# Query projections in two full column blocks instead of four padded ones, moved to their partitions by DMA

## The chip, the core and the metric

The kernel runs on one NeuronCore of a Trainium2 chip. Five engines work from instruction queues of their own: TensorE (PE, with its weight loads shown as PEld), VectorE (DVE), ScalarE (ACT), GpSimd (POOL) and SyncE (SP), which issues most of the DMAs. The metric is the device time of one execution, in microseconds (us). "Span" is the time from the first to the last instruction in the profiler's record of one execution.

## What is computed

The reference is one transformer layer in float32, with layer norms after each half: attention with 16 query heads and 4 key-value heads, then a mixture of 8 experts (one for each token) beside a shared one. Two sequences of 1024 tokens, 256 channels.

```python
q = (x @ Wq).reshape(B, T, N_HEAD, HEAD_DIM).transpose(0, 2, 1, 3)      # B 2, T 1024, 16 heads of 16
k = (x @ Wk).reshape(B, T, N_HEAD_KV, HEAD_DIM).transpose(0, 2, 1, 3)   # 4 heads of 16, repeated 4 times
v = (x @ Wv).reshape(B, T, N_HEAD_KV, HEAD_DIM).transpose(0, 2, 1, 3)
att = jnp.einsum('bhqd,bhkd->bhqk', q, k) * scale + alibi[None] + causal[None, None]
y = jnp.einsum('bhqk,bhkd->bhqd', jax.nn.softmax(att, axis=-1), v)
x = _layernorm(x + y.transpose(0, 2, 1, 3).reshape(B, T, C) @ Wo)
# each token goes to the expert with the largest logit; xr is x times its sigmoid
x = _layernorm(x + silu(x @ sh_gate) * (x @ sh_up) @ sh_down
                 + (up(xr) * silu(gate(xr))) @ down_proj)
```

## The kernel before

**Layout of queries and keys.** A head has 16 numbers, but a score matmul works on a quadrant of 32 partitions. Quadrant g (partitions 32 g to 32 g + 31) belongs to key-value head g. Row 0 of a quadrant carries the position term: the query side holds the head's slope (qbias), the key side the position (kaug). Row 1 is for the row maximum, rows 16 to 31 hold the head's 16 numbers. qT is 128 partitions x 4 (r, the query head within its group) x 1024 tokens; kT is 128 x 1024. To get this layout straight out of a matmul, the weights are padded: wq_pad (L129) has, for each r, 4 groups of 32 columns of which 16 are filled, so that one r gives 128 columns; wk_pad is the same for the keys.

**Projections by halves.** A half is 512 tokens of one batch; there are four. For each half, turn_x (L305) transposes x into xT with 8 matmuls and one copy on ScalarE; do_kv (L316) projects keys and values, and VectorE adds kaug (L330) and ScalarE copies the values (L331); do_q (L333) projects the queries for two values of r, and ScalarE writes them with the bias into qT (L338). So a half takes two calls of do_q, and each writes two blocks of 128 columns, in two matmuls each. All of these tiles, and those of the scores, come from one PSUM pool, ps_st, with 3 buffers of two banks.

**Order.** On PE, VectorE, ScalarE and GpSimd the order in the attention part is that of the program text (MANUAL); on SP it is a scheduler's there, and the program's in the expert part. Ahead of the attention part stands a setup, which a scheduler orders: the loads, the padded weights, rowsel, slopes, qbias and kaug (L147 to L158).

**Stages of the attention part.**

- first_projections (L354): two matmuls of zeros, the transposes of the first half, do_kv and both calls of do_q for it, and turn_x of the second half.
- Ten lead steps (LEAD): each computes the scores of one unit (start_s, two bursts of matmuls, L401) and reduces them to row maxima (end_s: VectorE on L416, L425 and L444, ScalarE on L432 with GpSimd on L433). They cover the query tiles 0 to 3 of batch 0. Between them stand pieces of the projections of the other three halves, taken from the list of projections() (L342) by weight: after step k, pieces are taken until their share left is at most (9 - k) / 10.
- The main steps: for each query tile and key tile, transposed scores with the maximum subtracted (t_ps, L481), exponentials on ScalarE (L500), the product with the values (L524), and one unit of scores further on; join_maxima and spread_maxima (L451, L461) bring the maxima from the one to the other, with qS = qT + mT on VectorE (L469).
- The shared expert (sh_gu, sh_d) and the routing fill the end of it; routed rows are scattered into slot_x in DRAM. Then comes the expert part.

**Loads.** On SP in this order: x (xs, four parts), wo, the router, the shared expert's weights (L110 to L112, 1.5 MB) and a fill of slot_x with an empty row (L281, 3.9 MB). ScalarE issues those of Wq, Wk and Wv.

**Buffers.** The pool "probT" has four buffers under the tag pT, 8 KB a partition, for probabilities; xT of batch 1 takes one of them until its projections are done.

Of the kernel before, what the change touches and what calls it, by code (L numbers as in the profile page):

```python
# [9 lines left out]
F32 = mybir.dt.float32  # L10
# [6 lines left out]
P = 128  # L17
# [13 lines left out]
    mybir.EngineType.DVE,  # L31
    mybir.EngineType.Activation,
    mybir.EngineType.Pool,
}


# [8 lines left out]
def attn_moe_postln_kernel(  # L45
# [61 lines left out]

    sh_gu = const.tile([P, KC, F2], F32, tag="sh_gu", name="sh_gu")
    sh_d = const.tile([P, FC, C], F32, tag="sh_d", name="sh_d")
    nc.sync.dma_start(out=sh_gu[:, :, :FF], in_=sh_gate.rearrange("(c p) f -> p c f", p=P))  # L110
    nc.sync.dma_start(out=sh_gu[:, :, FF:], in_=sh_up.rearrange("(c p) f -> p c f", p=P))
    nc.sync.dma_start(out=sh_d, in_=sh_down.rearrange("(c p) n -> p c n", p=P))  # L112

# [9 lines left out]

    wq_pad = acon.tile([P, KC, REP, N_KV, PAD], F32, tag="wq_pad", name="wq_pad")
    wk_pad = acon.tile([P, KC, N_KV, PAD], F32, tag="wk_pad", name="wk_pad")  # L129
    nc.vector.memset(wk_pad, 0.0)  # L130
    nc.vector.memset(wq_pad, 0.0)
    for c in range(KC):
        nc.vector.tensor_scalar_mul(
            wq_pad[:, c, :, :, ROW_HEAD : ROW_HEAD + HD],
            wq_raw[:, c, :].rearrange("p (g r d) -> p r g d", g=N_KV, d=HD),
            scale,
        )
        nc.vector.tensor_copy(
            wk_pad[:, c, :, ROW_HEAD : ROW_HEAD + HD],
            wk_raw[:, c, :].rearrange("p (g d) -> p g d", d=HD),  # L140
        )
# [121 lines left out]
    with (  # L263
# [11 lines left out]
    ):  # L275
        qT, kT, xT = {}, {}, {}

        empty = shp.tile([P, ROW], F32, tag="th", name="empty")
        nc.gpsimd.memset(empty, 0.0)
        nc.gpsimd.memset(empty[:, NUM : NUM + 1].bitcast(I32), NTT * P)  # L280
        nc.sync.dma_start(out=slot_xt, in_=empty.unsqueeze(1).broadcast_to([P, SLOTS // P, ROW]))  # L281


        def pj_tile(name):
            return ps_m.tile([P, 512], F32, tag="m", name=name)
# [1 line left out]
        def own_tiles(b, xTb):  # L287
            xT[b] = xTb
            kT[b] = qkp.tile([P, T], F32, tag="kT", name=f"kT_{b}")
            qT[b] = qkp.tile([P, REP, T], F32, tag="qT", name=f"qT_{b}")  # L290

        def project(dst, b, w, cols):
            for c in range(KC):
                nc.tensor.matmul(  # L294
                    dst, lhsT=w(c), rhs=xT[b][:, c, cols], start=(c == 0), stop=(c == KC - 1)
                )

        def wq_of(r):
            return lambda c: wq_pad[:, c, r].rearrange("p g d -> p (g d)")

        def wk_of(c):
            return wk_pad[:, c].rearrange("p g d -> p (g d)")
# [2 lines left out]
        def turn_x(b, i):  # L305
            if b not in xT:

                xTb = ptp.tile([P, KC, T], F32, tag="pT", name=f"xT_{b}")
                own_tiles(b, xTb)
            tp = ps_st.tile([P, KC, 512], F32, tag="st", name="xtp")  # L310
            for c in range(KC):
                for j in range(4):
                    nc.tensor.transpose(tp[:, c, ts(j, P)], xs[:, b * QT + i + j, ts(c, P)], ident)
            nc.scalar.copy(xT[b][:, :, i * P : (i + 4) * P], tp)
# [15 lines left out]
            nc.vector.tensor_add(kT[b][:, cols], pj[:, 0], kaug[:, cols])  # L330
            nc.scalar.copy(vs[b][:, i : i + 4, :, 0:HD], pv)  # L331

        def do_q(b, r, i):  # L333
            cols = slice(i * P, (i + 4) * P)
            pj = ps_st.tile([P, 2, 512], F32, tag="st", name="qpj")
            for j in range(2):
                project(pj[:, j], b, wq_of(r + j), cols)
            nc.scalar.activation(qT[b][:, r : r + 2, cols], pj, AF.Identity, bias=qbias)  # L338

        halves = [(b, i) for b in range(B) for i in range(0, QT, 4)][1:]  # L340

        def projections():  # L342


            pieces = []
            for h, after in zip(halves, [*halves[1:], None]):
                pieces.append((11, lambda h=h: do_kv(*h)))
                pieces.append((14, lambda h=h: do_q(h[0], 0, h[1])))
                if after:
                    pieces.append((4, lambda h=after: turn_x(*h)))  # L350
                pieces.append((14, lambda h=h: do_q(h[0], 2, h[1])))
            return pieces

        def first_projections():  # L354

            own_tiles(0, xTp.tile([P, KC, T], F32, tag="xT", name="xT_0"))
            cols = slice(0, 512)
            warm = ps_st.tile([P, 2, 512], F32, tag="st", name="warm")
            zeros = mnegs[0].rearrange("p r g d -> p (r g d)")
            for i in range(2):  # L360
                nc.tensor.matmul(warm[:, i], lhsT=zeros[:, :P], rhs=zeros, start=True, stop=True)
            tp = ps_st.tile([P, KC, 512], F32, tag="st", name="xtp0")
            for c in range(KC):
                for j in range(4):
                    nc.tensor.transpose(tp[:, c, ts(j, P)], xs[:, j, ts(c, P)], ident)
            nc.scalar.copy(xT[0][:, 0, cols], tp[:, 0])
            nc.vector.tensor_copy(xT[0][:, 1, cols], tp[:, 1])
            do_kv(0, 0)
            do_q(0, 0, 0)
            do_q(0, 2, 0)  # L370
            turn_x(*halves[0])


        def s_units(b, qt):
# [464 lines left out]
        for k in range(LEAD):  # L839
            unit = s_queue.pop(0)  # L840
            sps = [start_s(unit, h) for h in range(2)]
            run(*[m for _, m in sps])
            for h in range(2):
                end_s(unit, h, sps[h][0], h == 1)
            while fill and left * LEAD > total * (LEAD - 1 - k):
                left -= fill[0][0]
                fill.pop(0)[1]()
            gap(0)
        for n, (b, qt, kt) in enumerate(steps):
            last = n + 1 == len(steps) or steps[n + 1][:2] != (b, qt)  # L850
            made = []
            if kt != qt:
                made.append((2 * n + 2, (b, qt, kt, kt == 0, False)))
            if last:
                ready = max(2 * n + 2, 2 * first[b, qt] + (7 if qt >= 3 else 4))
                made.append((ready, (b, qt, qt, qt == 0, True)))
            if s_queue:
                unit = s_queue.pop(0)
                for h in range(2):
                    t = start_t(b, qt, kt, h)  # L860
                    s = start_s(unit, 1 - h)
                    run(t[1], s[1])
                    end_t(b, qt, kt, h, t[0])
                    end_s(unit, 1 - h, s[0], h == 1)
                    if h == 1:
                        products += made
                    gap(6)
            else:

                t = [start_t(b, qt, kt, h) for h in range(2)]  # L870
                run(t[0][1], t[1][1])
                for h in range(2):
                    end_t(b, qt, kt, h, t[h][0])
                products += made
                wide_gap()
# [13 lines left out]
    with (  # L889
# [6 lines left out]
        tc.tile_pool(name="ps_d", bufs=2, space=PSUM) as ps_d,  # L896
        tc.tile_pool(name="ps_t", bufs=2, space=PSUM) as ps_t,
        tc.tile_pool(name="rt2", bufs=1) as rtp,
        tc.manual_schedule(engines=MANUAL | {mybir.EngineType.SP}),
    ):  # L900
        wgu = wgup.tile([P, E, KC, F2], F32, tag="wgu", name="wgu")
        wd = wgup.tile([P, E, FC, C], F32, tag="wd", name="wd")
# [386 lines left out]
```

## Time and profile before

| | us |
|---|---|
| median of 3 runs | 615.26 (612.56 to 615.57) |
| the profiled execution, its time | 613.16 |
| the profiled execution, its span | 611.4 |
| span from 0 to 19.8: setup and first projections, PE busy | 16.3 of 19.8 |
| 19.8 to 71.5: lead steps, PE / DVE / ACT busy | 49.6 / 31.0 / 16.1 of 51.7 |
| 71.5 to 350: main steps, PE / DVE / ACT busy | 272.9 / 194.3 / 167.1 of 278.5 |
| 350 to 460: last steps and shared expert, PE busy | 102.7 of 110.0 |
| 460 to the end: expert part, PE busy | 133.1 of 151.4 |

A busy share says how long an engine had an instruction at work, and matmuls are pipelined, so that a busy PE may still be waiting within an instruction. What decides a stage is which wait ends last there; that is read from the chain, which follows each piece of work back to what released it. In the views of the chain and the timeline, a line has its start, its length (both us), the engine, the tile and the line of the kernel, and the number of instructions. In the groups, a line has the count, the total busy us and the mean ns of one, then the idle time ahead of it and what ended most of that.

### The profile page before, as it was taken

The numbers are of one execution on the slowest core, as the hardware profiler recorded it, in microseconds if no ns is written. First come the engines' busy times: TensorE is split into PE (matmuls) and PEld (weight loads), VectorE is DVE, ScalarE is ACT, GpSimd is POOL, SyncE is SP. The second block draws the span as 40 slices with busy tenths as digits, with TensorE's granted clock in tenths as the row PEclk, the third lists the DMA queues.
The fourth block names the chain that finished last, engine by engine and source line by source line (L and its number), as shares of the span: only waits on it lengthen the run. The fifth ranks groups of instructions, "written<-read, shape, count | busy, mean of one in ns | idle before, by whom it ended". The sixth has DMA issues, their size and how long they took to land.

```text
span 611.4 us, 9157 instructions
## 1 busy us (share of the span) xinstructions
PE 574.6 (94%) x3708; PEld 321.0 (53%) x3708; DVE 334.0 (55%) x606; ACT 253.5 (41%) x313; POOL 155.2 (25%) x189
## 2 busy tenths in 40 slices
PE   7999999999999999999999999998989999999990
PEld 4555434444445353435355634545554788888660
DVE  3275667857675766676766834343442254454541
ACT  1423476565665655646465664453112111111120
POOL 3010222111111102013312120222102147767541
PEclk9999989999999999999999999999999999999996
DMA  9700000000000000001100000100053345752100
GB/s 310 236 1 2 1 0 2 2 1 1 1 1 2 1 1 0 3 0 36 36 1 2 2 0 1 52 19 18 17 206 102 118 177 177 260 198 69 57 22 4
DMA packets 23102, 32.65 MB, mean 53 GB/s; under 512 B 3294, under 2 KB 18948, under 8 KB 23056
## 3 DMA queue, kind: packets, MB, share of 16 engines
q1 hardware_dynamic: 18784, 25.28, 12.5%
q0 software_dynamic: 3456, 6.34, 3.0%
q8 instruction: 31, 0.51, 0.4%
q10 hardware_dynamic: 816, 0.39, 0.2%
q14 instruction: 15, 0.12, 0.1%
HBM read 22.20 MB, written 12.97 MB: 58 GB/s over the span
## 4 chain that ended last, share of the span: by engine, by line
PE 84%; DVE 6%; ACT 5%; issue 1%; DMA 1%; POOL 0%; POOLq 0%; ACTq 0%
PE t_ps L481 15%; PE s_ps L401 12%; PE yT L524 11%; PE gu_sh L683 6%; PE qpj L294 5%; PE gp L1100 5%; PE dp L1116 5%; PE up L1100 5%; PE dp_sh L703 3%; ACT pT L500 3%; PE o_ps L569 2%; DVE past L416 2%; PE mT L465 1%; PE dp L1158 1%; PE gp L1008 1%
## 5 line engine op out<-in xcount | busy, mean ns | idle before, releaser
L416 DVE TENSOR_REDUCE past<-s_ps 128x2 f32<-128x1024 f32 (+2 forms) x112 | 136.5, 1223 | 71.2 <-PE s_ps L401 71.0
L401 PE MATMUL s_ps<-kT,qT 32*128 32x128 f32 (+2 forms) x1280 | 154.0, 379 | 4.2 <-ACT pT L500 2.0
L500 ACT ACTIVATE pT<-t_ps 128x1024 f32<-128x1024 f32 x112 | 113.9, 1025 | 94.5 <-PE s_ps L401 59.8
L481 PE MATMUL t_ps<-qS,kT 32*128 32x512 f32 x576 | 149.0, 633 | 0.9 <-DVE qS L469 0.8
L401 PEld LDWEIGHTS s_ps<-kT,qT 32*128 32x128 f32 x1280 | 79.9, 185 | 36.2 <-ACT pT L500 25.2
L481 PEld LDWEIGHTS t_ps<-qS,kT 32*128 32x128 f32 x576 | 41.3, 183 | 52.0 <-issue 30.1
L504 POOL TENSOR_SCALAR_AFFINE_SELECT pD<-pD 128x1024 f32<-128x1024 f32 x32 | 34.7, 1091 | 103.2 <-ACT pD L502 103.1
L524 PE MATMUL yT<-pT,v 128*32 128x512 f32 x448 | 59.7, 605 | 0.0
L433 POOL TENSOR_SCALAR_AFFINE_SELECT diag<-diag 128x1024 f32<-128x1024 f32 x16 | 17.5, 1091 | 135.4 <-ACT diag L432 123.0
L233 POOL TENSOR_TENSOR rstd<-rstd,neg_half 128x1 f32<-128x1 f32 x36 | 20.5, 570 | 121.5 <-DVE rstd L232 119.4
L683 PE MATMUL gu_sh<-x1T,sh_gu 128*128 128x512 f32 x96 | 43.8, 598 | 1.9 <-DVE h_sh L695 1.3
L239 POOL DMA_INDIRECT slot_x<-xs,slots x32 | 32.1, 1002 | 43.7 <-DVE slots L664 27.7
L502 ACT COPY pD<-t_ps 128x1024 f32<-128x1024 f32 x32 | 32.1, 1017 | 25.6 <-PE s_ps L401 19.9
L444 DVE TENSOR_REDUCE past<-diag 128x8 f32<-128x1024 f32 x32 | 38.6, 1210 | 0.0
L516 ACT ACTIVATE pD<-pD 128x1024 f32<-128x1024 f32 x32 | 33.6, 1056 | 0.3 <-POOL pD L504 0.3
L1108 ACT ACTIVATE sg<-gp 128x512 f32<-128x512 f32 x16 | 9.6, 597 | 54.6 <-PE gp L1100 47.1
L692 DVE SCALAR_TENSOR_TENSOR h_sh<-th,gu_sh 128x512 f32<-128x512 f32 x12 | 8.3, 688 | 43.0 <-ACT th L691 43.0
L1100 PE MATMUL gp<-slot_xT,wgu 128*128 128x256 f32 x128 | 30.4, 381 | 1.2 <-ACT slot_xT L1069 1.2
L1100 PE MATMUL up<-slot_xT,wgu 128*128 128x256 f32 x128 | 30.2, 379 | 0.0
L294 PE MATMUL qpj<-xT,wq_pad 128*128 128x512 f32 x64 | 29.2, 602 | 0.6
L1116 PE MATMUL dp<-wd,slot_h 128*128 128x256 f32 x128 | 29.0, 379 | 0.0
L683 PEld LDWEIGHTS gu_sh<-x1T,sh_gu 128*128 128x128 f32 x96 | 17.4, 190 | 20.4 <-issue 17.2
(170 smaller groups left out, 675.2 us busy)
## 6 DMA issues: line engine op xcount, KB each, us to landing
wgu<-_L_ffn_gate_up_proj_dram SPq DMA_DIRECT2D x8, 1024.0 KB
wd<-in_L_ffn_down_proj_dram SPq DMA_DIRECT2D x8, 512.0 KB
slot_x<-empty SPq DMA_DIRECT2D x1, 3900.0 KB
row<-slot_x SPq DMA_DIRECT2D x8, 260.0 KB
xs<-in_L_attn_x_dram SPq DMA_DIRECT2D x4, 512.0 KB
z_dram<-z_sh SPq DMA_DIRECT2D x12, 128.0 KB
row<-slot_x SPq DMA_DIRECT2D x4, 130.0 KB
sh_gu<-L_ffn_shared_gate_w_dram SPq DMA_DIRECT2D x1, 512.0 KB
```

The source lines that it names most:

```text
L294: nc.tensor.matmul(dst, lhsT=w(c), rhs=xT[b][:, c, cols], start=(c == 0), stop=(c == KC - 1))
L401: lambda r=r, j=j, rows=rows: nc.tensor.matmul(sp[:, j, r * n * P : (r + 1) * n * P], lhsT=qT[b][rows, r0 + r, ts(qt, P)], rhs=kT[b][rows, ...
L416: nc.vector.tensor_reduce(past[:, gs, r0 : r0 + nr, parts[b, qt][key]], sp.rearrange("p j (r k) -> p j r k", r=nr), AX.X, ALU.max, negate= ...
L444: lambda: nc.vector.tensor_reduce(past[:, gs, :, 0], diag[:, gs], AX.X, ALU.max, negate=True),
L481: lambda j=j, rows=rows: nc.tensor.matmul(tp[:, j, :], lhsT=kT[b][rows, ts(kt, P)], rhs=qS[b, qt][rows].rearrange("p r q -> p (r q)"), sta ...
L500: nc.scalar.activation(p, tp, AF.Exp)
L504: nc.gpsimd.affine_select(out=p, in_=p, pattern=[[0, HALF * REP], [1, P]], compare_op=ALU.is_ge, fill=MASKED, base=0, channel_multiplier=-1,)
L516: lambda: nc.scalar.activation(p, p, AF.Exp),
L524: nc.tensor.matmul(yTs[b, qt][g * PAD : (g + 1) * PAD], lhsT=vs[b][:, kt, g, :], rhs=p[:, g, :], start=start, stop=stop,)
L683: nc.tensor.matmul(gu[:, k], lhsT=sh_gu[:, c, col : col + P], rhs=x1T[:, c, ts(tb, TB)], start=(c == 0), stop=(c == KC - 1),)
L1100: nc.tensor.matmul(dst[:, j], lhsT=wgu[:, e, c, col : col + P], rhs=xT[:, c, :], start=(c == 0), stop=(c == KC - 1),)
L1116: nc.tensor.matmul(dp, lhsT=h[:, f, ts(i, P)], rhs=wd[:, e, f, :], start=(f == 0), stop=(f == FC - 1),)
```

## The change

The query weights lose their padding: wq_r holds, for each value of r, 4 groups of 16 columns, so that two values of r make one block of 128 columns. do_q projects a half's queries in one call of two such blocks. Their rows come out as (r, g, 16 numbers), not in the quadrants of qT. They are copied to an SBUF tile (stage, a pT buffer; in the first half ScalarE and VectorE copy one block each), and eight DMAs on SP, one for each of two r and four g, bring 16 partitions each to rows 16 to 31 of quadrant g in qT. The bias row and the zero rows of qT are written beforehand, by a copy of qbias over the whole tile, 512 tokens at a time: by ScalarE for the first half, by GpSimd for the others (own_tiles).

In first_projections the query projection comes ahead of do_kv, and do_kv of the second half is added at its end. The list of pieces has one call of do_q a half, and do_kv of the second half is out of it. The loads of the shared expert's weights and the fill of slot_x, with the two GpSimd memsets that it needs, are issued after the lead steps. SP follows the program's order in the attention part too.

```diff
@@ -31,6 +31,7 @@
     mybir.EngineType.DVE,
     mybir.EngineType.Activation,
     mybir.EngineType.Pool,
+    mybir.EngineType.SP,
 }
 
 
@@ -107,9 +108,6 @@
 
     sh_gu = const.tile([P, KC, F2], F32, tag="sh_gu", name="sh_gu")
     sh_d = const.tile([P, FC, C], F32, tag="sh_d", name="sh_d")
-    nc.sync.dma_start(out=sh_gu[:, :, :FF], in_=sh_gate.rearrange("(c p) f -> p c f", p=P))
-    nc.sync.dma_start(out=sh_gu[:, :, FF:], in_=sh_up.rearrange("(c p) f -> p c f", p=P))
-    nc.sync.dma_start(out=sh_d, in_=sh_down.rearrange("(c p) n -> p c n", p=P))
 
 
 
@@ -125,13 +123,13 @@
 
 
 
-    wq_pad = acon.tile([P, KC, REP, N_KV, PAD], F32, tag="wq_pad", name="wq_pad")
+
+    wq_r = acon.tile([P, KC, REP, N_KV, HD], F32, tag="wq_r", name="wq_r")
     wk_pad = acon.tile([P, KC, N_KV, PAD], F32, tag="wk_pad", name="wk_pad")
     nc.vector.memset(wk_pad, 0.0)
-    nc.vector.memset(wq_pad, 0.0)
     for c in range(KC):
         nc.vector.tensor_scalar_mul(
-            wq_pad[:, c, :, :, ROW_HEAD : ROW_HEAD + HD],
+            wq_r[:, c],
             wq_raw[:, c, :].rearrange("p (g r d) -> p r g d", g=N_KV, d=HD),
             scale,
         )
@@ -275,11 +273,6 @@
     ):
         qT, kT, xT = {}, {}, {}
 
-        empty = shp.tile([P, ROW], F32, tag="th", name="empty")
-        nc.gpsimd.memset(empty, 0.0)
-        nc.gpsimd.memset(empty[:, NUM : NUM + 1].bitcast(I32), NTT * P)
-        nc.sync.dma_start(out=slot_xt, in_=empty.unsqueeze(1).broadcast_to([P, SLOTS // P, ROW]))
-
 
         def pj_tile(name):
             return ps_m.tile([P, 512], F32, tag="m", name=name)
@@ -288,6 +281,10 @@
             xT[b] = xTb
             kT[b] = qkp.tile([P, T], F32, tag="kT", name=f"kT_{b}")
             qT[b] = qkp.tile([P, REP, T], F32, tag="qT", name=f"qT_{b}")
+            for i in range(0, T, 512):
+
+                copy = nc.scalar.copy if b == 0 and i == 0 else nc.gpsimd.tensor_copy
+                copy(qT[b][:, :, i : i + 512], qbias.unsqueeze(2).broadcast_to([P, REP, 512]))
 
         def project(dst, b, w, cols):
             for c in range(KC):
@@ -295,8 +292,8 @@
                     dst, lhsT=w(c), rhs=xT[b][:, c, cols], start=(c == 0), stop=(c == KC - 1)
                 )
 
-        def wq_of(r):
-            return lambda c: wq_pad[:, c, r].rearrange("p g d -> p (g d)")
+        def wq_of(m):
+            return lambda c: wq_r[:, c, 2 * m : 2 * m + 2].rearrange("p r g d -> p (r g d)")
 
         def wk_of(c):
             return wk_pad[:, c].rearrange("p g d -> p (g d)")
@@ -330,12 +327,27 @@
             nc.vector.tensor_add(kT[b][:, cols], pj[:, 0], kaug[:, cols])
             nc.scalar.copy(vs[b][:, i : i + 4, :, 0:HD], pv)
 
-        def do_q(b, r, i):
+        def do_q(b, i):
+
+
             cols = slice(i * P, (i + 4) * P)
+            stage = ptp.tile([P, N_KV, 512], F32, tag="pT", name="q_all")[:, :2]
             pj = ps_st.tile([P, 2, 512], F32, tag="st", name="qpj")
-            for j in range(2):
-                project(pj[:, j], b, wq_of(r + j), cols)
-            nc.scalar.activation(qT[b][:, r : r + 2, cols], pj, AF.Identity, bias=qbias)
+            for m in range(2):
+                project(pj[:, m], b, wq_of(m), cols)
+            if (b, i) == (0, 0):
+                nc.scalar.copy(stage[:, 0], pj[:, 0])
+                nc.vector.tensor_copy(stage[:, 1], pj[:, 1])
+            else:
+                nc.scalar.copy(stage, pj)
+            to = qT[b].rearrange("p (m r) t -> p r m t", r=2)
+            for r in range(2):
+                for g in range(N_KV):
+                    row = (r * N_KV + g) * HD
+                    nc.sync.dma_start(
+                        out=to[g * PAD + ROW_HEAD : g * PAD + ROW_HEAD + HD, r, :, cols],
+                        in_=stage[row : row + HD],
+                    )
 
         halves = [(b, i) for b in range(B) for i in range(0, QT, 4)][1:]
 
@@ -344,11 +356,11 @@
 
             pieces = []
             for h, after in zip(halves, [*halves[1:], None]):
-                pieces.append((11, lambda h=h: do_kv(*h)))
-                pieces.append((14, lambda h=h: do_q(h[0], 0, h[1])))
+                pieces.append((14, lambda h=h: do_q(*h)))
                 if after:
                     pieces.append((4, lambda h=after: turn_x(*h)))
-                pieces.append((14, lambda h=h: do_q(h[0], 2, h[1])))
+                if h != halves[0]:
+                    pieces.append((11, lambda h=h: do_kv(*h)))
             return pieces
 
         def first_projections():
@@ -365,10 +377,10 @@
                     nc.tensor.transpose(tp[:, c, ts(j, P)], xs[:, j, ts(c, P)], ident)
             nc.scalar.copy(xT[0][:, 0, cols], tp[:, 0])
             nc.vector.tensor_copy(xT[0][:, 1, cols], tp[:, 1])
+            do_q(0, 0)
             do_kv(0, 0)
-            do_q(0, 0, 0)
-            do_q(0, 2, 0)
             turn_x(*halves[0])
+            do_kv(*halves[0])
 
 
         def s_units(b, qt):
@@ -846,6 +858,16 @@
                 left -= fill[0][0]
                 fill.pop(0)[1]()
             gap(0)
+
+        nc.sync.dma_start(out=sh_gu[:, :, :FF], in_=sh_gate.rearrange("(c p) f -> p c f", p=P))
+        nc.sync.dma_start(out=sh_gu[:, :, FF:], in_=sh_up.rearrange("(c p) f -> p c f", p=P))
+        nc.sync.dma_start(out=sh_d, in_=sh_down.rearrange("(c p) n -> p c n", p=P))
+
+        empty = shp.tile([P, ROW], F32, tag="th", name="empty")
+        nc.gpsimd.memset(empty, 0.0)
+        nc.gpsimd.memset(empty[:, NUM : NUM + 1].bitcast(I32), NTT * P)
+        nc.sync.dma_start(out=slot_xt, in_=empty.unsqueeze(1).broadcast_to([P, SLOTS // P, ROW]))
+
         for n, (b, qt, kt) in enumerate(steps):
             last = n + 1 == len(steps) or steps[n + 1][:2] != (b, qt)
             made = []
@@ -896,7 +918,7 @@
         tc.tile_pool(name="ps_d", bufs=2, space=PSUM) as ps_d,
         tc.tile_pool(name="ps_t", bufs=2, space=PSUM) as ps_t,
         tc.tile_pool(name="rt2", bufs=1) as rtp,
-        tc.manual_schedule(engines=MANUAL | {mybir.EngineType.SP}),
+        tc.manual_schedule(engines=MANUAL),
     ):
         wgu = wgup.tile([P, E, KC, F2], F32, tag="wgu", name="wgu")
         wd = wgup.tile([P, E, FC, C], F32, tag="wd", name="wd")
```

## The prediction

> **What bounds the kernel now.** First the page, for who is busy: PE in every slice, and the chain that ends last is 84% PE, with the query projections among its parts.
>
> ```profile
> PE 574.6 (94%) x3708; PEld 321.0 (53%) x3708; DVE 334.0 (55%) x606; ACT 253.5 (41%) x313; POOL 155.2 (25%) x189
> PE 84%; DVE 6%; ACT 5%; issue 1%; DMA 1%; POOL 0%; POOLq 0%; ACTq 0%
> L294 PE MATMUL qpj<-xT,wq_pad 128*128 128x512 f32 x64 | 29.2, 602 | 0.6
> ```
>
> Reader: 64 records for 8 calls of do_q, so 8 a call; their ends overlap, and a call holds PE 3.43 us (below: 6.92 for two).
>
> Second, the chain over the start, 0 to 21 us.
>
> ```profile
> 1.29 5.74 DMA wk_raw<-in_L_attn_Wk_dram
> ...
> 7.06 0.30 DVE wk_pad L138 x2
> ...
> 7.73 0.72 DVE kaug L158
> 8.45 0.06 DVE qbias L153
> 8.52 0.61 DVE xT L367
> 9.13 0.04 issue
> 9.17 1.12 PE kvpj L294 x2
> 10.29 1.73 PE kvpj L323 x16
> 12.03 6.92 PE qpj L294 x16
> 18.95 0.88 PE xtp L313 x8
> ```
>
> VectorE takes everything behind the landing of wk_raw; qbias is ready only at 8.5. The first score burst (S0) starts at 19.8.
>
> Third, the chain from 17 to 76 us, the ten lead steps.
>
> ```profile
> 31.94 1.18 DVE past L416
> 33.12 0.04 issue
> 33.16 3.71 PE qpj L294 x8
> 36.88 0.02 issue
> 36.90 1.12 ACT qT L338
> 38.02 0.04 issue
> 38.07 1.99 PE kvpj L294 x4
> ```
>
> Every query block is on it. PE to ACT to PE means one of the three PSUM pairs ("st") is returned. They go round in program order: a score burst takes two, a projection or turn one.
>
> **The skill.** "DMA: Bandwidth & Descriptors", Anatomy of one DMA: about 2 us fixed for a transfer, mostly the receipt. No row of before is a transfer inside SBUF; SP's issue of a load is 0.35 to 0.6 us there. "SBUF — State Buffer", Door 1: 16 partitions reach 4 of 16 ports, 104 GB/s measured. "TensorE: Matmul & The Clock Gate", Part 1: an idle window of 3.4 us can halve the clock. The trace agrees on the cold side: the first L361 records take 0.86 us where L294 ones take 0.43. "SBUF — State Buffer", Who interferes with whom: tensor_reduce never contends with GpSimd; the trace can't show it yet.
>
> **Projections.** Four heads of 16 columns padded to 32 filled a 128-column block; now eight fill it, so a half needs two blocks instead of four. Eight do_q of 3.43 become four: -13.7 us of PE. In the first half that is -3.43, in the lead -10.3. One more kv projection (3.47: 1.72 + 1.75) goes from the lead to before S0.
>
> **The start.** In after, ACT's first work is the fill of qT: 128x2048 from qbias. From the COPY rows (512 in 0.585, 1024 in 1.01) a 2048 copy is 1.87. It waits for qbias, 8.5, and behind it in ACT's order stands the copy of xT's first half, at 6.48 in before. So: fill 8.55 to 10.45, xT to 11.05, PE idle since 6.44. I take VectorE's order as before: the removed memset of wq_pad (0.91) lay in the wait for wq_raw. Then do_q 11.05 to 14.5, do_kv to 18.0, turn_x to 19.05. The added do_kv needs that turn's xT: ACT 1.1, so it runs 20.2 to 23.7; rps, and S0 at 23.9: +4.1 against 19.8.
>
> **Transfers.** The stage copies (0.58 ACT, 0.68 DVE, side by side) end at 15.25. SP issues eight transfers of 64 KB at 0.45, to 18.9; with 2.2 for the last one's landing (2 fixed, 0.6 by 104 GB/s lying partly in it) 21.1. That is 2.8 inside S0's 23.9, hence free. Cover gone: each transfer would have to hold the queue 0.8 instead of 0.45. Bounds: below 0 is excluded, since S0 waits for PE anyway; above, 1.5 each gives S0 at 29.5 (+5.6). SP also waits eight DMAs back: rw_raw is issued at 4.97, 1.2 after the issue before it, on wq_raw by SP's list of waits. By 15.3 the loads are down, as the later ones (sh, slot_x) now come after the lead. The other 24 transfers serve queries not read in the lead, and nothing on SP is due then.
>
> **The lead.** ACT's evacuations go from six of 1.11 to three of 1.01. I lay the instructions out with before's durations (S 1.15, reduces L416 1.22 and L444 1.21, diag 1.22, do_kv 3.47, turn 1.05), the three PSUM pairs and the new list. Costs now sum to 72, so steps 0 to 8 take q(0,4); turn(1,0); q(1,0); none; turn(1,4); kv(1,0); q(1,4); none; kv(1,4). Times from S0's start: S0 0 to 1.2; q to 4.65; S1 to 5.8; turn to 6.9; S2 to 8.3; q to 11.75; S3 to 12.95. S4 waits for S3's diag on VectorE, 14.5. Turn to 16.7; S5 waits for S4's reduce, 18.15; kv 19.3 to 22.75; S6 to 23.9; q to 27.4; S7 to 28.55; S8 waits, 29.85; kv 31.1 to 34.55; spread_maxima; S9 35.2 to 36.4. VectorE: 12 reduces of scores (14.7), 8 of diag (9.7), 4 diag (4.9), two kT, one qS and two joins (2.4): 31.7 (the trace has 31.0 in 19.8 to 71.5); its waits (1.25 at S0, 3.4 for S1 behind q, 1.1 for kv, 2.7 for S7) 8.4: join at 40.1. In before the second join ends at 71.5, 51.7 after S0. So the lead gives 51.7 - 40.1 = 11.6: of 13.8 taken from PE (10.3 and 3.5), 2.2 goes to waits for VectorE, late next.
>
> **GpSimd and the rest.** Three fills of 2048, by its affine_select (1024 in 1.09) about 2.1 each; up to 4.4 each if twice as slow. The two of batch 1 start at about 8 after S0 and end by 12.3 (17 at worst); the next diag select comes at 14.1, and its result is reduced only at 23.5: free. Tiles of pT for stages: four buffers, first probabilities after the lead: free. Late loads: sh_gu is read from 355, slot_x scattered into at about 275; 5.4 MB took some 20 us in before: free. From the main steps on the order is the same, and PE is busy 48.8 of 50 us, so what the lead ends earlier is the end earlier.
>
> **Sum.** +4.1 - 11.6 = -7.5. The profiled execution has a span of 611.4 and a time of 613.16: it would have 605.7. The median, 615.26, is 2.1 above it; the same step from it gives 607.8. I forecast 608.
>
> **Rivals.** (1) qbias comes early: ident is ready at 3.24, so if VectorE takes rowsel, slopes and qbias before the weights, the fill ends at about 6.2 and xT's copy is not late. q then ends at 10.7, S0 starts at 20.1, gain 11.3: 604. Against it: VectorE sat idle until 5.06 with ident ready at 3.24 and still took wk_pad first. (2) PE's pause (4.6 us) or the thinner lead costs the clock. For: the page's PEclk falls to 8 around 80 us. Half speed for one or two windows is 1.7 to 3.4, and as much in the lead where VectorE doesn't cover it: gain 3 to 5, 611. (3) VectorE binds the lead harder, or the first steps at 70 to 90 us fall into a worse phase: gain under 3, 614. To lose 4.5 more, PE would have to stall half a step in each of ten. (4) Slower: the transfers. If each holds the queue for its whole life instead of being issued over the last, S0 comes at 15.25 + 8p + 2. It passes 23.9 at p = 0.8; the gain is gone when S0 is 7.5 later, p = 1.8; slower by over 3 us from p = 2.1. At p = 2.3 S0 is at 35.7, and the time 615.3 - 7.5 + 11.8 = 620. For: a fixed 2 us each, few ports, eight waits of PE on eight transfers. Against: SP issued loads 0.5 apart without waiting for landings. (5) The change doesn't do as it says: a score burst could wait for transfers into other columns of qT. In before S3 starts at 36.79 while ACT writes other columns of qT from 36.90, so reads are kept apart by region; I give it nothing of its own.
>
> **Numbers.** Forecast 0.50, (1) 0.14, (2) 0.13, (3) 0.09, (4) 0.14. A measurement of this kernel tells 0.5% from nothing, about 3 us. Faster: 0.50 + 0.14 + 0.13 = 0.77; same 0.09; slower 0.14. The range leaves out (4) and the edges of (1): 602.5 to 615. The likeliest case's own range is 605 to 611 (profiled time or median as the base; 2 us of clock or landing).
>
> **What would show it.** Right: qpj with 32 records; S0 at 23 to 25 us with PE, not a DMA, before it; the fill of qT on ACT from 8.5 to 10.4; S0 to the second join some 40 us; VectorE named ahead of S4, S5, S8; from there to the end as before. Wrong: s_ps waiting on DMA qT, 128x512 records of 0.86 after 11 us, a fill at 4 us (rival 1), or a main part longer than before.

## The result, and the profile after

The changed kernel takes 608.07 us (median of 4 runs, 607.72 to 609.49) where the kernel before, measured beside it, takes 615.41 (4 runs, 612.56 to 616.83). The ratio is 0.9891, 95% interval 0.9852 to 0.993: some 7 us faster, as forecast. The profiled execution of after took 608.26 us with a span of 606.6.

The page of after, its busy times, the granted clock of TensorE over 40 slices of some 15 us, the chain by engine and the issues of the new transfers:

```profile
PE 566.0 (93%) x3676; PEld 318.6 (53%) x3676; DVE 333.5 (55%) x606; ACT 250.3 (41%) x310; POOL 161.2 (27%) x192
...
PEclk8999799999999999999999999999999999999997
...
PE 82%; DVE 6%; ACT 5%; issue 2%; DMA 1%; SPq 1%; POOL 0%; POOLq 0%; ACTq 0%; DVEq 0%
...
qT<-q_all SPq DMA_DIRECT2D x32, 64.0 KB, 2.3
```

PE has 32 matmuls fewer: 8 instead of 16 for each of four halves. That is the removed work, and PE is 8.6 us less busy. The clock has two dips ahead of the kernel's last slice: 8 in the first, 7 in the fifth, at 61 to 76 us.

The chain over the start of after (start, length in us, then what):

```profile
8.58 0.07 DVE qbias L151
8.66 0.02 issue
8.68 1.90 ACT qT L287
10.58 0.49 ACT xT L378
11.07 0.04 issue
11.11 5.11 PE qpj L291 x8
16.22 1.72 PE kvpj L291 x4
17.94 1.75 PE kvpj L320 x16
...
20.49 0.37 ACT v L328
20.86 0.92 ACT xT L311
21.79 0.04 issue
21.83 1.98 PE kvpj L291 x4
23.81 1.73 PE kvpj L320 x16
25.55 0.15 PE rps L846
25.70 1.05 PE s_ps L413 x29
```

The path is the one that the prediction laid out: qbias, the fill of qT, xT, queries, keys, the second half's turn, its keys, the first scores (S0). No DMA stands ahead of s_ps. But the query projection takes 5.11 us instead of the 3.43 it was priced at. The stretches of two us around it say why (length, then busy time and count for PE, PEld, DVE, ACT, POOL, then the clock, DMA share and GB/s):

```profile
8.00:10.00 2.00, 0.00 (x0) 0.00 (x0) 0.65 (x2) 1.32 (x1) 1.29 (x1) 1.00 1.05 368
10.00:12.00 2.00, 0.89 (x1) 0.50 (x2) 0.69 (x1) 1.06 (x2) 0.85 (x2) 0.64 0.03 9
12.00:14.00 2.00, 2.00 (x4) 0.84 (x3) 0.00 (x0) 0.00 (x0) 0.00 (x0) 0.51 0.00 0
14.00:16.00 2.00, 2.00 (x6) 0.86 (x5) 0.00 (x0) 0.00 (x0) 0.00 (x0) 1.00 0.00 0
```

PE has nothing to do from 7.3 to 11.1, and the clock is at half for 3.4 us, from 10.6 to 14.0 (hence the means of 0.64 and 0.51). Now the three stages, cut at S0 and at the end of the second join of row maxima, which starts the main steps, first before, then after:

```profile
0.00:19.77 19.77, 16.26 (x58) 8.41 (x58) 4.82 (x16) 4.14 (x5) 6.02 (x24) 1.00 0.96 316
19.77:71.50 51.73, 49.59 (x407) 29.30 (x406) 31.02 (x31) 16.11 (x18) 4.83 (x5) 1.00 0.14 41
71.50:611.40 539.90, 508.71 (x3246) 283.32 (x3246) 298.14 (x560) 233.30 (x291) 144.30 (x161) 0.99 0.13 45
```

```profile
0.00:25.55 25.55, 18.85 (x72) 10.93 (x73) 4.75 (x16) 5.54 (x6) 7.63 (x23) 0.93 0.45 129
25.55:65.20 39.65, 36.53 (x362) 22.57 (x362) 30.52 (x31) 11.24 (x13) 8.41 (x8) 1.00 0.34 69
65.20:606.60 541.40, 510.66 (x3247) 285.10 (x3246) 298.19 (x559) 233.53 (x291) 145.15 (x161) 0.98 0.16 53
```

So the start lost 5.8, the lead gave 12.1, the main part lost 1.5: -4.8 = 606.6 - 611.4. The last column but two, the granted clock, is the key to the third stage. Two stretches of it:

```profile
66.00:68.00 2.00, 2.00 (x22) 1.73 (x22) 1.06 (x2) 0.00 (x0) 0.29 (x1) 0.50 1.04 341
...
72.00:78.00 6.00, 5.77 (x21) 1.58 (x21) 3.53 (x4) 4.93 (x6) 2.19 (x2) 0.50 1.09 334
```

Altogether 10.2 us run at half speed between 65 and 79 us; in the profiled execution of before it was 3.4, at 79.6 to 83.0. The DMA engines are full in these stretches too: here the late loads (5.4 MB) land. Which of the two costs the 1.5 us was a question for the runs.

Towards the end of the lead, from 54.2 to 61.0, the chain of after names issues of SP and a landing of qT, and the page counts 1% for SP. That is not a wait: at 61.0 VectorE goes on without a pause from one instruction (kT, 60.40 to 61.09) to the next (past L456, from 61.00), and the landing only falls at the same time.

### The profile page after: what moved, and what is told of

Same layout as the page of the kernel before. It is cut to its first block, busy times and chain, and to the rows that moved or that the text cites. A ratio compares the mean times of both kernels' runs of the same rounds, so it can differ in the third digit from the quotient of the medians.

```text
span 606.6 us, 9162 instructions
## 1 busy us (share of the span) xinstructions
PE 566.0 (93%) x3676; PEld 318.6 (53%) x3676; DVE 333.5 (55%) x606; ACT 250.3 (41%) x310; POOL 161.2 (27%) x192
## 4 chain that ended last, share of the span: by engine, by line
PE 82%; DVE 6%; ACT 5%; issue 2%; DMA 1%; SPq 1%; POOL 0%; POOLq 0%; ACTq 0%; DVEq 0%
PE t_ps L493 16%; PE s_ps L413 12%; PE yT L536 11%; PE gu_sh L695 6%; PE gp L1122 5%; PE dp L1138 5%; PE up L1122 5%; PE dp_sh L715 3%; PE qpj L291 3%; ACT pT L512 3%; PE o_ps L581 2%; PE mT L477 1%; PE dp L1180 1%; DVE past L428 1%; PE gp L1030 1%
## 5 line engine op out<-in xcount | busy, mean ns | idle before, releaser
L413 PE MATMUL s_ps<-kT,qT 32*128 32x128 f32 (+2 forms) x1280 | 157.4, 383 | 5.0 <-ACT pT L512 1.8
L493 PE MATMUL t_ps<-qS,kT 32*128 32x512 f32 x576 | 150.9, 641 | 1.8 <-DVE qS L481 1.8
L413 PEld LDWEIGHTS s_ps<-kT,qT 32*128 32x128 f32 x1280 | 81.4, 187 | 37.2 <-ACT pT L512 24.7
L493 PEld LDWEIGHTS t_ps<-qS,kT 32*128 32x128 f32 x576 | 42.0, 186 | 53.3 <-issue 31.7
L456 DVE TENSOR_REDUCE past<-diag 128x8 f32<-128x1024 f32 x32 | 38.6, 1211 | 0.0
L1122 PE MATMUL gp<-slot_xT,wgu 128*128 128x256 f32 x128 | 30.4, 381 | 1.2 <-ACT slot_xT L1091 1.2
L695 PEld LDWEIGHTS gu_sh<-x1T,sh_gu 128*128 128x128 f32 x96 | 17.4, 190 | 20.4 <-issue 17.2
L1067 POOL DMA_INDIRECT zt<-z_dram,row x20 | 20.6, 1032 | 27.8 <-issue 27.2
```

The source lines that it names most:

```text
L413: lambda r=r, j=j, rows=rows: nc.tensor.matmul(sp[:, j, r * n * P : (r + 1) * n * P], lhsT=qT[b][rows, r0 + r, ts(qt, P)], rhs=kT[b][rows, ...
L456: lambda: nc.vector.tensor_reduce(past[:, gs, :, 0], diag[:, gs], AX.X, ALU.max, negate=True),
L493: lambda j=j, rows=rows: nc.tensor.matmul(tp[:, j, :], lhsT=kT[b][rows, ts(kt, P)], rhs=qS[b, qt][rows].rearrange("p r q -> p (r q)"), sta ...
L695: nc.tensor.matmul(gu[:, k], lhsT=sh_gu[:, c, col : col + P], rhs=x1T[:, c, ts(tb, TB)], start=(c == 0), stop=(c == KC - 1),)
L1122: nc.tensor.matmul(dst[:, j], lhsT=wgu[:, e, c, col : col + P], rhs=xT[:, c, :], start=(c == 0), stop=(c == KC - 1),)
```

## The experiments

Two theories. **The first** is the prediction's with a clock added: the start is set by the fill of qT on ScalarE and by a pause that halves the clock; the transfers lie beside PE's work; the lead gives what PE no longer does, less waits for VectorE; the main part differs by its clock alone. **The rival** puts the start down to the transfers and the loss in the main part to the load burst. Except where a run says otherwise each edit is to the changed kernel, and S0 and the second join are read from the run's chain and groups (S0 with the two short rps matmuls just ahead of it).

**The fill of the first half on GpSimd too (e1).**

```diff
-                copy = nc.scalar.copy if b == 0 and i == 0 else nc.gpsimd.tensor_copy
-                copy(qT[b][:, :, i : i + 512], qbias.unsqueeze(2).broadcast_to([P, REP, 512]))
+                nc.gpsimd.tensor_copy(qT[b][:, :, i : i + 512], qbias.unsqueeze(2).broadcast_to([P, REP, 512]))
```

> The changed kernel with the fill of qT for the first half on GpSimd too, so that ScalarE's copy of xT no longer stands behind it. Theory 1 (the fill on ScalarE holds the first query projection): xT's copy starts as soon as the transposes end, near 7.4 us instead of 10.5, the first q matmul near 8, the second operand's at 9.4, PE makes no pause over 2 us and its clock stays full. q ends near 12, the two stage copies one after the other by 13.4, eight transfers by 18.6, the last lands at 20.9; S0 at 21.2 to 21.6 instead of 25.6. Time 4 us under the changed kernel's 608.1: 604. Theory 2 (S0 waits for the transfers, not for PE): S0 moves with the transfers' end too, but is then named as waiting for a DMA, and starts at 21 to 23. Theory 3 (something else sets the start, such as the landing of the weights): S0 stays within 1 us of 25.6 and the time at 608.

603.81 us (6 runs, 602.56 to 605.35), ratio 0.9826 (0.9798 to 0.9855). The chain at its start:

```profile
8.44 0.07 DVE qbias L151
8.50 0.61 DVE xT L378
9.11 0.04 issue
9.15 2.84 PE qpj L290 x6
...
21.47 1.06 PE s_ps L412 x29
```

ScalarE copies its part of xT at 6.57, PE starts at 7.2, and only VectorE's part (its constants first) is late. S0 comes 4.2 us earlier than in after (21.3), and the clock stays at 1.00 up to there; the ratio falls by 0.0065, 4.0 us. So the fill on ScalarE was worth some 4 us, part of it through the clock (the next run separates them). GpSimd takes 1.89 us for the same fill.

**PE kept at work in the pause (e2).** Four more matmuls of zeros behind the transposes.

```diff
+            for i in range(4):
+                nc.tensor.matmul(warm[:, i % 2], lhsT=zeros[:, :P], rhs=zeros, start=True, stop=True)
             nc.scalar.copy(xT[0][:, 0, cols], tp[:, 0])
```

> The changed kernel with four more matmuls of zeros into the warm-up tile, in PE's pause between the first transposes and the first query projection; the order on the other engines is as in the changed kernel. Theory 1 (the pause of PE, 3.8 us, costs the clock): the records of the first query block take 0.43 us instead of 0.64 on average, q takes 3.43 instead of 5.11, S0 comes 1.7 earlier, at 23.9, if the transfers allow it (stage copies at 15.9, issue to 21.1, landing 23.4). Time 606.4. Theory 2 (the slow records have another cause, the rest of the loads for example): q takes 5.1 us again, S0 at 25.6, 608. The slow clock at 65 to 79 us should not change in either.

606.28 us (6 runs, 604.01 to 607.94), ratio 0.9863 (0.9832 to 0.9894). The one line that counts:

```profile
10.96 3.70 PE qpj L291 x8
```

The fill stays where it was, the queries wait for it as long, the path stays, and the query projection falls from 5.11 to 3.70 us; S0 is at 24.0 (prediction: 23.9). So the clock lost in the pause was 1.4 us of the start. This is read from the trace; the intervals of the two ratios overlap. The half-speed stretch behind the lead stays (13.7 us in 64 to 78).

**The late loads issued first again (e3).** The three loads of the shared expert and the fill of slot_x, with its memsets, moved from behind the lead to ahead of first_projections().

```diff
+        nc.sync.dma_start(out=sh_gu[:, :, :FF], in_=sh_gate.rearrange("(c p) f -> p c f", p=P))
...
+        nc.sync.dma_start(out=slot_xt, in_=empty.unsqueeze(1).broadcast_to([P, SLOTS // P, ROW]))
+
         first_projections()
```

> The changed kernel with the loads of the shared expert's weights and the fill of slot_x issued ahead of the first projections, as in the kernel before. Theory 1 (the move of the loads is what keeps the first transfers short): the transfers are issued late, since each waits for the transfer eight back, and they share the DMA engines with the 5.4 MB until about 26 us; the last lands at 28 to 31, S0 follows it at 28 to 31 instead of 25.6, PE or VectorE waits for a DMA of qT, and the time is 3 to 5 us over the changed kernel's 608.1, at 611 to 613. Theory 2 (small transfers slip between the packets of the large ones): S0 stays at 26 and the time at 608. For the slow clock from 65 to 79 us: if the burst of loads at 62 to 79 causes it, it is gone here; if PE's own short pauses at the end of the lead do, it stays.

615.02 us (22 runs, 613.62 to 617.07), ratio 1.0014 (0.9999 to 1.0029): the whole gain is gone. Its chain, and from the waits of SP's queue the one line (us in total, times, longest):

```profile
16.13 1.38 PE kvpj L291 x4
17.51 9.98 DMA qT<-q_all
27.49 0.14 issue
27.63 4.41 PE s_ps L413 x31
```

```profile
SPq L347 <- DMA slot_x<-empty: 2.0, 1, 2.0
```

Here the transfers are what the rival says they are. One of them waits 2.0 us in SP's queue for the fill of slot_x, and the eight take 10.2 us to issue instead of 5.2. The first is down 10.0 us after its issue began, where after needs 2.3 to 2.5. The first scores start at 27.63 instead of 25.70, and their burst takes 4.4 us instead of 1.1, since it goes on waiting for the later transfers, the last of which lands at 30.4. PE's pause ahead of it is followed by half speed from 27.6 to 34.4. The second join is 6.4 us later. The loss is 7 us where 3 to 5 were expected; 6.8 us at half speed can be at most 3.4 of it, and how it divides between waits and clock wasn't separated. And the half-speed stretch behind the lead is there (10.2 us in 72 to 86) although the DMA engines are idle then: it does not need the load burst.

**The late loads alone (e4).** The kernel before with those loads moved behind its lead and SP in the program's order, nothing else.

```diff
+    mybir.EngineType.SP,
...
-    nc.sync.dma_start(out=sh_d, in_=sh_down.rearrange("(c p) n -> p c n", p=P))
...
+        nc.sync.dma_start(out=sh_d, in_=sh_down.rearrange("(c p) n -> p c n", p=P))
```

> The kernel before with one part of the change alone: the loads of the shared expert's weights and the fill of slot_x issued after the lead steps, SP in program order. Theory 1 (nothing in the old start waits for these loads): within 0.3% of before, S0 at 19.8, the second join at 71.5. Theory 2 (they compete with the first loads): wk_raw lands up to 1 us sooner than 7.03 and all follows, 1 us gained. If the burst of loads at the lead's end causes the slow clock, the slow stretch of about 4 us at 79 to 84 us gets longer here and 1 to 2 us are lost.

614.22 us (14 runs, 613.26 to 616.45), ratio 1.0008 (0.9989 to 1.0027); S0 at 20.0. The profiled execution has 6.8 us at half speed behind the lead where that of before has 3.4, which is what was expected if the load burst costs clock; it is one execution of each, and e3 and e5 speak against the burst. By itself the move is worth nothing; without it the new projections are worth nothing. The two parts of the change are one.

**Half as much for VectorE in the lead (e8).** The reduces of the lead take half of each key block's columns; the maxima of the other half are left out.

```diff
-                    sp.rearrange("p j (r k) -> p j r k", r=nr),
+                    sp.rearrange("p j (r k) -> p j r k", r=nr)[
+                        :, :, :, : n * P // (2 if slot < 0 else 1)
+                    ],
```

> The changed kernel, where in the lead steps VectorE takes the maxima over the first half of each key block's columns only, so that its twelve reduces of scores there read 512 columns instead of 1024; the other half is left out of these maxima. They take 0.69 us instead of 1.22, 6.4 us of VectorE's work in all. Theory 1 (after the change VectorE is late in the lead): laid out with the shorter reduces, the stretch from S0 to the second join falls from 39.5 to 36.5, and the time by 3, to 605. Theory 2 (PE or ScalarE still sets the lead): the stretch falls by less than 1 us and the time stays at 608.

606.54 us (6 runs, 604.92 to 608.97), ratio 0.9887 (0.9853 to 0.992). From S0 to the second join it takes 36.9 us instead of 39.6, near the 36.5 expected; PE's program is the same. So VectorE's work sets 2.7 us of the lead's length. The profiled execution took 605.25, 3 us less than that of after (with 6.8 us at half speed in its start, S0 at 26.1); the median shows little of it, and where its other runs lose it wasn't seen.

**The clock behind the lead (e5).** e1 with matmuls of zeros: one of 512 columns behind the lead, one of 256 in each of the first six half steps. (The tile of zeros is set by GpSimd at the start.)

```diff
+        def keep(cols):
+            nc.tensor.matmul(
+                pj_tile("keep")[:, :cols], lhsT=zeros[:, :P], rhs=zeros[:, :cols], start=True, stop=True
+            )
...
+        keep(512)
...
                     run(t[1], s[1])
+                    if n < 3:
+                        keep(256)
```

> On top of the fill on GpSimd: matmuls of zeros in PE's waits at the end of the lead and in the first main steps, one of 512 columns (0.86 us) after the lead and one of 256 columns (0.43 us) in each of the first six half steps, 3.4 us in all, with a tile of zeros of their own. Theory 1 (PE's short waits there let its clock fall to half from 61 to 74 us): the half-speed stretch shrinks from 13 us to 3 or none, the time from the second join to the end falls from 541.7 to 540, and the time from 603.8 to 602 or a little more, as some zeros delay real work. Theory 2 (a running average over something longer, or the load of 32-row matmuls, sets the clock): the stretch stays over 10 us and the zeros cost 1 to 3 us: 605 to 607.

602.06 us (5 runs, 601.72 to 602.24), ratio 0.9805 (0.9774 to 0.9836). Two stretches, of e1 and then of e5:

```profile
65.00:70.00 5.00, 5.00 (x16) 2.02 (x14) 2.17 (x2) 4.85 (x6) 3.23 (x3) 0.50 1.09 337
```

```profile
65.00:70.00 5.00, 5.00 (x26) 1.66 (x20) 3.67 (x4) 5.00 (x6) 3.60 (x4) 1.00 1.09 335
```

The DMA engines are as full in both; PE is as busy by its records in both; the clock is 0.50 in one and 1.00 in the other, and PE gets through 26 matmuls instead of 16. From the second join to the end it is 541.7 us in e1 (13.7 at half speed), 539.2 here, with the zeros in it. Useless work made the profiled execution faster. The medians fall too, from 603.81 to 602.06, but the intervals of the two ratios overlap.

**The second half's transposes ahead of the keys (e6).** On e1.

```diff
             do_q(0, 0)
-            do_kv(0, 0)
             turn_x(*halves[0])
+            do_kv(0, 0)
             do_kv(*halves[0])
```

> On top of the fill on GpSimd: in the first projections the turn of the second half comes ahead of the first half's key and value projection, so that ScalarE copies xT while PE projects, and PE's wait of 2.1 us (15.5 to 17.6) is gone. If PE alone set S0, it would start at 19.3 instead of 21.4. Theory 1 (the transfers, 5.2 us of issue and 2.3 to the landing of the last, now end last): S0 starts at 20.9 to 21.1, with a DMA of qT named ahead of it, and the time is 0.4 under 603.8. Theory 2 (the transfers are not what S0 waits for): S0 at 19.3, time 601.7.

602.96 us (6 runs, 601.6 to 603.48), ratio 0.9816 (0.9787 to 0.9845). The chain:

```profile
11.99 0.87 PE xtp L309 x8
12.86 1.72 PE kvpj L290 x4
...
19.82 0.15 PE rps L845
19.97 1.39 PE s_ps L412 x28
```

ScalarE's copy of the second half now has the first half's keys as cover, and S0 starts at 19.8 instead of 21.3. But its burst takes 1.4 to 1.5 us instead of 1.06, since its second half waits for the last transfer, which is issued at 18.0 and lands at 20.4. The second join gains 1.2 us, between the two theories: the start of S0 does not depend on the transfers, its end does.

**Two queues (e7).** e6 with four of the first eight transfers issued by ScalarE.

```diff
-                    nc.sync.dma_start(
+                    queue = nc.scalar if (b, i) == (0, 0) and r == 1 else nc.sync
+                    queue.dma_start(
```

> As the kernel with the turn first, and four of the first half's eight transfers issued by ScalarE, beside SP's four. Theory 1 (it is the issue, 0.65 us each on one queue, that makes the transfers last): both queues are done at 16.1 and the last transfer lands at 18.4; ScalarE's copy of xT stands behind its four issues, until 17, so S0 is at 19.5 to 20.2 and the time 1.2 to 1.9 under 603.8, at 602.2. Theory 2 (it is the moving of the bytes, 64 KB through few ports): the last lands at 20.9 as with one queue, S0 at 21.

602.7 us (6 runs, 600.2 to 603.89), ratio 0.982 (0.9791 to 0.9849).

```profile
13.70 2.68 DMA qT<-q_all
16.38 1.01 ACT xT L310
...
17.44 1.98 PE kvpj L290 x4
```

S0 comes at 21.2, near the second theory's 21 but by another path: the four issues hold ScalarE for 2.6 us, and its copy of xT comes at 16.4 instead of 12.9. (The line says DMA; it is the time in which ScalarE issued.) On the transfers themselves the second theory came nearer. The eight are issued by 16.6 instead of 18.6, but the last lands at 20.1, where it was 20.4 with one queue: each now takes 3.1 to 4.2 us to land instead of 2.3 to 2.5. So the issue is not all that limits them; what they share beyond it wasn't seen. This profiled execution happened to have no half-speed stretch at all, and needs 537.7 us from the second join to the end: the shortest of all profiled executions.

**Both gains, with zeros (e9) and with half as many (e10).** e6 with the lines of e5; in e10, 256 and 128 columns.

> The kernel of e6 with the multiplications of zeros of e5: both gains of the lead and a held clock. Theory 1 (the gains add, since one lies in the lead and the other behind it): first scores at 19.8 us, second join at 59.6, no half-speed stretch, clock 0.992 in every run, time 602.06 - 1.2 = 600.8 us within 0.5. Theory 2 (what the earlier turn gains is lost where the last transfers and the zeros meet on TensorE): time as e5, 602 us.

> As e9 with half as many zeros: 256 columns behind the lead, 128 in each of the first six half steps. Theory 1 (a small load is enough to hold the clock): clock 0.992, and since the zeros cost some 0.7 us rather than 1.5, 600.0 us. Theory 2 (the clock follows how full TensorE is, and this is too little): one or more half-speed stretches of 3.4 us come back between 59 and 80 us, and the runs spread over 601 to 603 us.

e9: 602.56 us (5 runs, 600.55 to 602.95), ratio 0.9804 (0.9776 to 0.9833). e10: 601.92 (5 runs, 600.05 to 602.49), ratio 0.9793 (0.9763 to 0.9823): the lowest ratio of all, though its interval holds those of e9 and e5. The profiled executions (600.55 and 600.4, clock 0.992) are as the first theory has them: S0 at 19.9 and 20.1, the second join at 59.8 and 60.0, no half speed behind it. But in each only two runs of five are there; the other three are some 2 us longer at a clock of 0.989. These two ran on another chip than e5 did, and there the zeros held the clock in only part of the runs, with the full amount no more than with half of it.

**The kernel before, and the change, at full clock (e11, e12).** e11 is the kernel before with the lines of e5 alone. e12 is the changed kernel with those lines and those of e2.

> The kernel before with the same zeros as e5, and nothing else. Theory 1 (the spread of the kernel before, 611 to 617 us, is half-speed stretches behind the lead): the clock is 0.992 in every run, the spread falls below 0.6 us, and the time is 611.0 + 1.5 for the zeros = 612.5 us. Theory 2 (the spread has another cause, in transfers for instance): runs from 611 to 617 us remain, at any clock.

> The changed kernel with the zeros in the pause of its start (as e2) and behind the lead (as e5): its start and its main part at full clock. Theory 1: first scores at 24.0 us, 39.5 us from there to the second join, clock 0.992 in every run, 604.6 us; against the kernel before with the same zeros this is the change at equal clock: +4.2 at the start, -12.0 in the lead, -7.5 to -8 us in all. Theory 2 (part of what the lead gains is given back in the main part whatever the clock): only -5 us between the two.

e11: 612.75 us (22 runs, 612.22 to 614.57), ratio 0.9984 (0.9968 to 1.0). e12: 606.31 (5 runs, 604.52 to 606.52), ratio 0.9864 (0.9836 to 0.9893). The kernel before had 27 runs beside them from 611.05 to 618.41, in steps: six below 611.7, nine from 612.7 to 613.8, eleven from 615.2 to 616.1, one at 618.4. With the zeros two steps are left: fifteen runs from 612.22 to 613.16 and seven from 613.94 to 614.57. So the spread falls from 7.4 to 2.4 us and not below 0.6: most of it went with the half-speed stretches that the zeros prevent. What remains shows a lower clock too: the mean of a run is 0.990 to 0.993 in the fifteen and 0.987 to 0.990 in the seven, and 3.4 us at half speed lower it by 0.003. So some half-speed time that the zeros did not prevent is likely there. Where it lies wasn't seen, as the profiled executions were clean ones, and the mean can't tell: every profiled execution also ends at half speed, for its last 9 to 12 us.

These profiled executions, both at 0.992, are the pair that differs by the change alone, but for e2's four matmuls of zeros in e12's start. First e11, then e12:

```profile
19.90 0.15 PE rps L836
20.06 1.34 PE s_ps L401 x30
```

```profile
24.08 0.15 PE rps L850
24.23 1.05 PE s_ps L415 x28
```

S0 is 4.2 us later (24.08 - 19.90); from there to the end of the second join 51.7 us (71.58 - 19.90) become 39.6 (63.71 - 24.08), -12.1; the rest, 539.2 and 539.1, is the same. In all -8.0, as the spans say (602.8 and 610.8). By steps of the runs, the medians of each: 604.8 against 612.6, and 606.4 against 614.1, -7.8 in both (two and three runs of e12). Nothing of the lead's gain is given back.

## Why the prediction was right, and where its sizes were off

The time, the sign and the main path came as forecast. By its own steps:

- **The projections.** qpj has 32 records; PE is 8.6 us less busy, where 13.7 were removed (the 3.5 of the added do_kv only moved to the start). The difference of 5.1 is what half speed explains: ahead of the kernel's end it lasts 13.7 us instead of 3.4, and half of the 10.2 more is 5.1. Right in kind.
- **The start, +4.1; measured +5.8, and +4.2 at full clock.** The step mis-sized is "do_q 11.05 to 14.5": it was priced with the full clock and took 5.11. The clock stood in the text as rival 2 and as the Trainium skill's ("TensorE: Matmul & The Clock Gate", Part 1: an idle window of some 3.4 us can halve it), with the pause put at 4.6 us, and yet the sum used the warm price. A pause of 3.8 us was enough here: 5.11 with it, 3.70 with zeros in it (e2), against 3.43. So where such a pause stands in the working, the work behind it is to be priced at half speed.
- **The fill, 1.87; measured 1.90,** at 8.68 instead of 8.55. Rival 1, qbias early, was wrong for the reason given: VectorE took wk_pad first.
- **The transfers, hidden by 2.8 us; measured 1.0.** Two terms were too small. The stage copies ran one after the other (ScalarE 16.26 for 0.59, then VectorE, waiting for it, 16.88 for 0.69) where they were put side by side; SP's issue of a transfer recurs every 0.65 us, not 0.45, and eight take 5.2 us. A third was too large: a landing takes 2.3 us from the start of its issue, where the working put 2.2 behind the end of the last issue. That estimate took the 2 us of fixed time that the Trainium skill gives ("DMA: Bandwidth & Descriptors", Anatomy of one DMA) for transfers issued by GpSimd; these were issued by SP, and their 2.3, with the moving of the bytes in it, is near that. The last landed at 24.5, S0 is at 25.55. What kept them hidden is the wait for ScalarE's turn of the second half: in e6, which takes that out of the path, the second half of S0 waits for the last of them.
- **Rival 4, transfers that set S0,** did not come true in the changed kernel, and e3 shows what kept it away: the loads behind the lead. The prediction said that "by 15.3 the loads are down", naming their move as the reason; e3 confirms that step, and gives its price, 7 us.
- **The lead, -11.6; measured -12.1, and the same at full clock.** VectorE is busy for 30.5 us in it (31.7 in the working) and waits 9.1 (8.4). The waits were the ones named: VectorE's for S1 behind the queries (3.5; 3.4 in the working), PE's for VectorE's diag and past (0.8 and 1.0 in total). That VectorE is "late next" is what e8 shows.
- **GpSimd.** The fills take 1.89 us (2.1 in the working), free as said, and VectorE's reduces beside them 1.22 as before; that agrees with the Trainium skill ("SBUF — State Buffer", Who interferes with whom).
- **The rest, "the same"; measured +1.5 in the profiled pair.** At equal clock it is the same (e11, e12); what differs is half-speed time, 10.2 us against 3.4. The late loads are neither needed for it (e3 has none there, and the stretch) nor enough (e5 and e7 have them, and no stretch); that they add to it, as e4's one execution could mean, is not excluded. This is the step where rival 2 was partly right: in the profiled pair the gain is 4.8, within its 3 to 5.
- **The base.** The profiled execution of before was one of its better ones: 613.16 against a median of 615.41. That of after was no better than its median (608.26 and 608.07). So -4.8 between two executions is -7.3 between the medians. The prediction's second base, the median, gave 607.8 and came nearest. That is partly luck: its -7.5 was nearly right at equal clock (-8.0), but the start cost 1.7 us more and the main part 1.5 more than it said in the profiled pair, and the medians agree because most runs of the kernel before are slower than its profiled one.

What stays open: why PE, about as busy, is throttled behind the lead in one execution and not in the next, and where the remaining steps of e9 to e12 arise. The zeros show that more work for PE there prevents most of it; no run tells what exactly the clock follows.

## What to carry over

Where a moved start opens a pause ahead of PE, price the work behind it at half speed, and look whether a cheap idle engine can take the copy that opens it: here GpSimd's fill instead of ScalarE's was worth 4 us beside the 7 of the change itself. Many small transfers inside SBUF are cheap only behind other work and with their queue free: 0.65 us of issue each on the queue that issues them and 2.3 to land, so the large loads go behind them. A second queue hardly helped: from the first issue to the last landing 6.4 us (e7) instead of 7.0 (e6). Before comparing two profiled executions, look where each stands among its kernel's runs, and at its clock.

## What the runs showed of the hardware

The clock's half-speed stretches come in pieces of about 3.4 us (3.4, 6.8, 10.2 and 13.7 in different executions), and behind the lead PE is busy by the records for nearly all of them. The more of it there is behind the second join, the longer that part takes: none 537.7 us (e7), 3.4 us of it 539.9 (before), 6.8 us 540.9 (e4), 10.2 us 541.4 (after), 13.7 us 541.7 (e1). This goes with the steps in the kernel's times, but does not explain each: beside e11, runs of the kernel before with the same mean clock of 0.984 stand at 613.05 to 613.53 and at 615.41 to 616.08.

The first stretch behind the lead starts, in each of the executions that have one, right behind 3.4 us in which PE is idle for 0.7 to 1.1 us. But such an idle time is not enough. First e1, where 13.7 us at half speed follow, then e7, where none follows:

```profile
56.83:60.25 3.42, 2.37 (x43) 1.45 (x37) 3.42 (x5) 0.73 (x2) 0.00 (x0) 1.00 0.90 281
```

```profile
55.89:59.30 3.41, 2.36 (x41) 1.60 (x40) 3.29 (x4) 0.37 (x1) 0.00 (x0) 1.00 0.74 175
```

PE's busy share by the records, 69% in both, does not tell the two apart. Seven matmuls of zeros, which cost 1.2 us (the lower step of e11, 612.6, against the lowest of before, 611.4), took most of the spread away, in the five runs of e5 all but 0.5 us.
